# Two attention layers on one core: in layer 1, the k projection's left operands are loaded in one transfer at the start of a batch, and the next input's pieces move to other steps

## The chip, the cores and the metric

The kernel runs on one core of one Trainium2 chip. Its time is the device time of one execution in microseconds. It was timed in three runs; a profiled execution is a run of its own. Everything is in float32.

Five engines work at once and each runs its own instructions in order: TensorE (PE, matmuls; its weight loads are listed apart as PEld), VectorE (DVE), ScalarE (ACT), GpSimd (POOL) and SyncE (SP). SP computes nothing here: it issues nearly all DMAs, and a wait of one DMA holds up those behind it on SP. POOL issues a few DMAs of its own on another queue. All DMAs run on the core's 16 DMA engines.

## The reference

The input x is 8 images of 512 channels by 32 x 32 positions (T = 1024 tokens). Layer 0 is a group norm followed by an attention with 8 heads of 64 channels, a projection and a residual. Layer 1, in which the change lies, is, for each image:

```python
y = gn(x)                                            # group norm, 32 groups
q = einsum('oc,bct->bot', w_q, y)  # k and v likewise, then split in 8 heads of 64
attn = einsum('bhdq,bhdT->bhqT', q, k) * scale       # scores per head
attn = einsum('gh,bhqT->bgqT', w_head, attn)         # heads are mixed, 8 x 8
attn = softmax(attn, axis=-1)
attn = (attn - mean) / sqrt(var + eps) * in_gamma + in_beta   # mean, var over one head's whole map
out = einsum('bhqT,bhdT->bhqd', attn, v).reshape(b, t, c)     # no transpose: rows of heads stand as tokens
x = x + (out @ w_proj.T + b_proj) transposed back to (b, c, h, w)
```

## The kernel before

**Layer 0** runs first, for all 8 images, and writes its result to DRAM (`x1_d`). It also prepares the left operands of layer 1's projections: a projection of 512 x 512 weights with 512 x 1024 inputs is split in 2 x 2 blocks and done with 7 block products in place of 8 (`Projection`, order 1, 6, 2, 7, 5, 3, 4), and each product has a left operand that is a block of the weights or a sum of blocks. The 7 left operands of one projection lie side by side in DRAM (`left_d`), 128 partitions x 14 KB, 1792 KB in all. The layer 1 part uses the left operands as matrices w_t[key][:, f] with f = 0 to 6: product 1 takes f = 0, product 2 f = 1, product 6 f = 4, product 7 f = 5, product 5 f = 3, product 3 f = 6, product 4 f = 2.

**Layer 1** takes one image (batch b = 0 to 7) after another. For one batch, `Attention1.step(p, t, ag)` runs steps p = 0 to 8 with four quarters t = 0 to 3. Step p computes the raw scores of 128 queries for all 8 heads and 1024 keys (`scores`, 8 calls i = 0 to 7 with kh = i // 4 the half of the keys; PE at L1701, copied out of PSUM by ACT at L1713 or, in p = 0, partly by DVE at L1711). A copy goes to a tile `raw[kh]`, and SP regroups it with DMAs of 256 KB into `re_t` (`regroup`, L1719), so that heads lie beside each other on partitions; 16 such DMAs a step, 8 for each half, issued in quarters 1 to 3 (half 0 in t = 1 and 2, half 1 in t = 3). Step p + 1 mixes the heads of these scores (`mix(p, s)`, s = 0 to 3, one each quarter; PE at L1738, two PSUM tiles each), and ACT takes the exponential of each tile (L1751). DVE transposes (`flip`, L1766) and takes moments (`moments`, L1780). Step p + 2 multiplies with v (`values`, L1796) and ACT stores the result (`leave`, L1812). So at any time three steps' work is interleaved on PE, in the order in which the code writes it: the engines' order is the program's (a manual schedule), and waits are derived from which regions of which tiles are read and written.

The scores and the mixes draw their PSUM tiles from one pool of three buffers in turn (`m_psum`, pool ps1_m; a tile is two banks). Quarter 3 of a step that has both scores and mixes is, in code:

```python
self.scores(p, 6)
if old:
    self.values(p - 1, 0, 0)
self.scores(p, 7)
if old:
    self.mix(p - 1, 3)
    self.values(p - 1, 0, 1)
```

Work beside this is put into slots. `ag` (an Agenda) holds functions by slot number, and step (p, t) runs slot 4p + t at its very end (so slot 26 is the end of p = 6, t = 2), with a few slots in between (such as 4p + 1.5) inside the step. Functions that matter here:

- `y_piece(b + 1, c)` (L1376): DMA of one 128-channel quarter (512 KB) of the next batch's input into the tile y, c = 0 to 3. The tile has one buffer, and the current y is read by v projections up to p = 1.
- `left_piece` (L1345) and `load_left` (L1355): DMAs of left operands into a tile `left` of a pool with one buffer, which the projections share in turn; within a batch it holds the k operands of the next batch, then, after the k projection, the q operands of the next batch. `left_p` loads the output projection's operands into a `raw` buffer instead.
- `normalize1(b + 1, c)` (slots 24 to 27): group norm of one quarter of the next y in place; odd c on ACT (L704), even c on DVE (L708).
- `right_y` (slot 31.5, POOL, L1393): sums of blocks of y that are right operands of the products; `k_go` (slots 31.5, 32.5, ...): the next batch's k projection, products 1, 2, 6, 7 in p = 8, and 5, 4, 3 after it. p = 8 has no scores of its own.
- `totals` in odd p: row sums of two steps, from which DVE takes reciprocals; POOL writes them to DRAM (zd, L1844) and, for the even p that follows, reads them back broadcast over partitions (rzb, L1856, two DMAs of 256 KB each), then divides (L1883).

After p = 8 a batch finishes its last values, the rest of the next k projection, the output projection (`out1`) and the next q projection (`q_projection(b + 1).run()`), which is the last call of a batch's loop body. In the last batch there is no next one; its pieces are four 256 KB quarters of the plain output weights (`p_piece`) instead, also one each step.

A list `a.pieces` holds the pieces of a batch, and a step that calls `self.piece()` takes the next one. In the kernel before that is every step from p = 2 on, at the end of t = 0, ahead of the slot that ends that quarter.

Of the kernel before, what the change touches and what calls it, by code (L numbers as in the profile page):

```python
# [467 lines left out]
def tile_two_attention_layers(  # L468
# [19 lines left out]
    nc = tc.nc  # L488
# [4 lines left out]
    NT = T // P  # L493
# [812 lines left out]
    with ExitStack() as l1:  # L1306
# [31 lines left out]
                [P, 7, 2 * HC], F32, tag="left", name=f"left_{key[0]}_{key[1]}"  # L1338
            )

        def left_piece(key, f, n):

            if f == 0:
                left_tile(key)
            nc.sync.dma_start(  # L1345
                out=w_t[key][:, f : f + n].rearrange("p f o -> p (f o)"),
                in_=left_d[key[0] + "1"][:, 2 * f * HC : 2 * (f + n) * HC],
            )

        def load_left(key, t=None):  # L1350
            if t is None:
                left_tile(key)
# [334 lines left out]
        class Attention1:  # L1687
# [242 lines left out]
            def step(self, p, t, ag):  # L1930

                new, old, older = p < NT, p >= 1, p >= 2
                if t == 0:
                    if new:
                        for i in range(3):
                            self.scores(p, i)
                            if i == 1:
                                ag.run(4 * p - 0.75)
                    if older:
                        self.values(p - 2, 0, 2, 3)  # L1940
                        self.leave(p - 2, 0)
                        if p % 2:
                            self.sums(p // 2 - 1)
                    ag.run(4 * p - 0.5)
                    k_leave()
                    if old:
                        self.mix(p - 1, 0)
                    ag.run(4 * p - 0.25)
                    if p % 2 == 0 and p >= 4:
                        self.broadcast(0)  # L1950
                elif t == 1:
                    if older:
                        self.values(p - 2, 1, 0)
                        self.flip(p - 1, 0)
                        if p % 2:
                            self.totals(p // 2 - 1)
                        self.moments(p - 1, 0)
                    if new:
                        self.scores(p, 3)
                    ag.run(4 * p + 0.5)  # L1960
                    k_leave()
                    if old:
                        self.mix(p - 1, 1)
                elif t == 2:
                    if p % 2 == 0 and p >= 4:
                        self.broadcast(1)
                    if older:
                        self.values(p - 2, 1, 1)
                    if new:
                        self.scores(p, 4)  # L1970
                        self.scores(p, 5)
                    ag.run(4 * p + 1.5)
                    k_leave()
                    if old and not new:
                        self.mix(p - 1, 2)
                    if older:
                        self.values(p - 2, 1, 2, 3)
                        self.leave(p - 2, 1)
                    if old and new:
                        self.mix(p - 1, 2)  # L1980
                else:
                    if new:
# [7 lines that stand above are left out]
                    else:  # L1990
                        ag.run(4 * p + 2.5)
                        k_leave()
                        self.mix(p - 1, 3)
                        self.values(p - 1, 0, 0, 1)
                if p == 1 or old and t:
                    self.flip(p - 1, t)
                    self.moments(p - 1, t)
                if new:
                    first = 3 + (p == 0)
                    for kh, s in (  # L2000
                        [], [(0, i) for i in range(first)], [(0, i) for i in range(first, 4)],
                        [(1, i) for i in range(4)],
                    )[t]:
                        self.regroup(p, kh, s)
                if t == 3 and p % 2 == 0 and p >= 4:
                    self.divide(p // 2 - 2, nc.gpsimd)
                if older and t == 0:
                    self.piece()
                ag.run(4 * p + t)

# [22 lines left out]
        for b in range(B):  # L2033
            more = b + 1 < B
            a = Attention1(b)
            ag = Agenda()
            j = 2 * NV
            for slot, i, cs in (
                (-0.75, j, (0, 1)), (1, j, (2, 3)), (1, j + 1, range(NCC)), (3, j + 2, range(NCC)),
                (3.75, j + 3, (0, 1)), (5.5, j + 3, (2, 3)),  # L2040
            ):
                ag.at(slot, lambda i=i, cs=cs: v_tile(b, i, cs))
            if b == 0:
                stages = group_stages(B - 1, B, small_psum1)
                for i in range(3):
                    ag.at(i, stages[i])
                ag.at(3, v_sums)
            if more:
                a.pieces += [lambda c=c: y_piece(b + 1, c) for c in range(NCC)]
                a.pieces += [lambda f=f: left_piece(("k", b + 1), f, 2) for f in (0, 4)]  # L2050
                ag.at(4 * NT, lambda: left_piece(("k", b + 1), 2, 2))
                ag.at(4 * NT, lambda: left_piece(("k", b + 1), 6, 1))
                for c in range(NCC):
                    ag.at(24 + c, lambda c=c: normalize1(b + 1, c))

                def k_go(*ms):
                    if not kp:
                        kp.append(k_projection(b + 1))
                    for m in ms:
                        kp[0].products(m)  # L2060
                        due.append(lambda m=m: kp[0].leave(m))

                kp = []
                ag.at(4 * NT - 0.5, lambda: right_tile(b + 1))
                ag.at(4 * NT - 0.5, lambda: k_go(1))
                ag.at(4 * NT - 0.5, lambda: right_y(b + 1))
                ag.at(4 * NT + 0.5, lambda: k_go(2))
                ag.at(4 * NT + 1, lambda: left_p(b))
                ag.at(4 * NT + 1.5, lambda: k_go(6))
                ag.at(4 * NT + 2.5, lambda: k_go(7))  # L2070
            else:
                a.pieces += [lambda c=c: p_piece(c) for c in range(NCC)]

                def prelude():
                    out_products.extend(out1_last(a))
                    out_products[0](0, [0, 1])

                out_products = []
                ag.at(4 * NT - 0.5, prelude)
            for p in range(NT + 1):  # L2080
                for t in range(4):
                    a.step(p, t, ag)
            ag.flush()
            k_leave()
            last = NT - 1
            a.sums(NCH - 1)
            if not more:
                a.values(last, 0, 2, 3)
                a.leave(last, 0)
                out_products[0](0, [2])  # L2090
                out_products[0](1, [0, 1])
                out_products[2]()
                a.values(last, 1, 0, 1, 2, 3)
                a.leave(last, 1)
                a.totals(NCH - 1)
                a.broadcast(0)
                a.broadcast(1)
                a.instance()
                out_products[1]()
                continue  # L2100
            k_go(5)
            a.values(last, 0, 2, 3)
            a.leave(last, 0)
            load_wv(b + 1)
            a.values(last, 1, 0, 1, 2, 3)
            a.leave(last, 1)
            a.totals(NCH - 1)
            a.broadcast(0)
            a.broadcast(1)
            a.instance()  # L2110
            k_leave()
            k_go(4, 3)
            k_leave()
            a.instance_end()
            v_pair(b + 1, 0)
            a.divide(NCH - 1)
            for g in range(H):
                a.affine(g)
            right_o = re_t[:, 4:8]
            combine_right(right_o, out_view(b))  # L2120
            op = out1(b, right_o)
            load_left(("q", b + 1))
            v_pair(b + 1, 1)
            a.check()
            op.run()
            q_projection(b + 1).run()
# [57 lines left out]
```

## Time and profile before

| | us |
|---|---|
| three timed runs | 3902.49, 3907.03, 3908.03; median 3907.03 |
| the profiled execution's own time | 3899.99 |
| its span, first to last instruction | 3898.1 |
| TensorE matmuls busy | 3845.0 (99% of the span) |
| VectorE / ScalarE / GpSimd busy | 2840.8 / 1962.0 / 207.4 |
| q1, the queue of SP's DMAs | 500.48 MB, 45.3% of 16 engines' span |

TensorE's clock was granted at 0.999 of full speed in this execution. Layer 1's first score matmul starts at 1778 us; a batch of layer 1 takes about 270 us, a step about 21 us. The page lists for each group of instructions its busy time, the mean duration of one, and then the time that its engine was idle just before them with what ended most of that wait. Idle time counts only on the engine that bounds the stage. The timeline rows give start and duration, the engine, the line, the operation, the tiles (out<-in), the shapes and, in brackets, idle time before the row and its releaser; a releaser is the signal that came last by the records, and of several that lie close together it can be the wrong one. In names of tiles, m is a mix's PSUM tile, s a score's, re the regrouped scores, e the exponentials, a the values' PSUM tile, pq and pk the q and k projections'.

### The profile page before, as it was taken

Reading aid. Unit: us, or ns where it says so; the run is one execution under the profiler, and the core shown is the slowest. Engines: PE = TensorE matmul, PEld = TensorE weight load, DVE = VectorE, ACT = ScalarE, POOL = GpSimd, SP = SyncE. Lnnn points to the kernel's source line nnn. Section 1 sums busy time; section 2 is a strip of 40 time slices with the busy share of each in tenths; the row PEclk is TensorE's granted clock in tenths of the full one; section 3 lists DMA queues with packets and bytes.
Section 4 is the critical chain, followed back from the end, with each engine's and each line's share of the span. In section 5 each row is a group of like instructions: output and inputs, shape, how many; then the busy total and the mean of one; then the engine's idle time right before and its main releaser. Section 6 shows DMA issues by size and latency. Waiting matters only on the chain. (4 is left out here: it accounts for less than half of the span.)

```text
span 3898.1 us, 95183 instructions
## 1 busy us (share of the span) xinstructions
PE 3845.0 (99%) x41612; PEld 1809.6 (46%) x41612; DVE 2840.8 (73%) x3921; ACT 1962.0 (50%) x2400; POOL 207.4 (5%) x210
## 2 busy tenths in 40 slices
PE   8999999999999999999999999999999999999999
PEld 4353535344353535344554544545545545445455
DVE  4858586675859485866967958859769668678598
ACT  1726354453627172534826717528438257176175
POOL 0000000000000000000110200201101102002000
PEclk9999999999999999999999999999999999999999
DMA  3313131111122121216947929749659479297385
GB/s 122 123 52 118 50 113 43 67 67 71 58 73 67 59 81 49 91 47 162 235 133 194 231 91 232 194 127 240 180 136 239 150 171 237 96 222 206 119 222 161
DMA packets 248440, 519.45 MB, mean 133 GB/s; under 512 B 49872, under 2 KB 57040, under 8 KB 241360
## 3 DMA queue, kind: packets, MB, share of 16 engines
q1 hardware_dynamic: 240832, 500.48, 45.3%
q0 software_dynamic: 7184, 12.81, 1.6%
q8 instruction: 328, 5.37, 0.6%
q14 instruction: 96, 0.79, 0.1%
HBM read 197.16 MB, written 46.92 MB: 63 GB/s over the span
## 5 line engine op out<-in xcount | busy, mean ns | idle before, releaser
L1766 DVE STREAM_TRANSPOSE et<-e 128x2048 f32<-128x2048 f32 x256 | 590.0, 2305 | 190.4 <-ACT e L1751 189.3
L1796 PEld LDWEIGHTS a<-et,v 128*64 128x64 f32 x16384 | 505.7, 138 | 283.8 <-issue 266.1
L1780 DVE BATCH_NORM_STATS2 bn<-e 128x6 f32<-128x512 f32 x1024 | 635.7, 683 | 0.0
L1107 ACT ACTIVATE e<-s 128x1024 f32<-128x1024 f32 x512 | 496.9, 1024 | 233.0 <-PE s L1102 233.0
L1713 ACT COPY raw<-s 128x1024 f32<-128x1024 f32 x480 | 470.1, 1018 | 224.8 <-PE s L1701 201.3
L1751 ACT ACTIVATE e<-m 128x1024 f32<-128x1024 f32 x512 | 496.2, 1021 | 165.7 <-issue 62.4
L1796 PE MATMUL a<-et,v 128*64 128x64 f32 x16384 | 553.3, 224 | 0.0
L1701 PE MATMUL s<-k,q 64*64 64x512 f32 x4096 | 513.2, 605 | 2.7 <-DVE v L1060 1.4
L1102 PE MATMUL s<-q,k 64*64 64x512 f32 x4096 | 490.4, 594 | 2.3 <-ACT e L1107 2.3
L1117 DVE TENSOR_TENSOR zacc<-zacc,e 128x1024 f32<-128x1024 f32 x384 | 467.5, 1217 | 27.2 <-ACT e L1107 1.4
L1130 PE MATMUL a<-e,v 64*64 64x512 f32 x4096 | 484.1, 589 | 0.0
L1738 PE MATMUL m<-re,wmix 32*32 32x512 f32 x8192 | 306.2, 599 | 14.8 <-DMA re<-raw 11.8
L1130 PEld LDWEIGHTS a<-e,v 64*64 64x64 f32 x4096 | 156.7, 133 | 282.8 <-issue 282.5
L1102 PEld LDWEIGHTS s<-q,k 64*64 64x64 f32 x4096 | 146.2, 133 | 284.4 <-issue 220.2
L1844 POOL DMA_DIRECT2D zd<-rz x96 | 52.5, 552 | 3361.9 <-DMA y<-x 1846.6
L1701 PEld LDWEIGHTS s<-k,q 64*64 64x64 f32 x4096 | 127.2, 132 | 216.0 <-issue 95.5
L1812 ACT COPY q<-a 64x256 f32<-64x256 f32 x256 | 94.0, 367 | 138.7 <-PE a L1796 137.1
L1738 PEld LDWEIGHTS m<-re,wmix 32*32 32x32 f32 x8192 | 68.1, 103 | 154.3 <-ACT raw L1713 65.9
L1509 PE MATMUL pv_t<-wv,y 128*128 128x512 f32 x256 | 120.6, 609 | 0.0
L920 PE MATMUL pv_p<-left_v,tmp 128*128 128x256 f32 x512 | 113.1, 379 | 0.0
L920 PE MATMUL pk_p<-tmp,left_k 128*128 128x512 f32 x256 | 112.5, 592 | 0.0
L920 PE MATMUL pq_p<-tmp,left_q 128*128 128x512 f32 x256 | 112.5, 592 | 0.0
(332 smaller groups left out, 3918.3 us busy)
## 6 DMA issues: line engine op xcount, KB each, us to landing
re<-raw SPq DMA_DIRECT2D x1024, 256.0 KB
left_q<-left_q SPq DMA_DIRECT2D x17, 1792.0 KB
left_p<-left_p SPq DMA_DIRECT2D x17, 1792.0 KB
left_k<-left_k SPq DMA_DIRECT2D x10, 1792.0 KB
x<-in_x_dram SPq DMA_DIRECT2D x32, 512.0 KB
rzb<-zd SPq DMA_DIRECT2D x128, 128.0 KB
x<-x SPq DMA_DIRECT2D x64, 256.0 KB
y<-x SPq DMA_DIRECT2D x32, 512.0 KB
```

Source lines behind the costliest of these rows:

```text
L920: nc.tensor.matmul(out, st, mv, start=start, stop=(k == 1), skip_group_check=True)
L1102: nc.tensor.matmul(ps[c * D : c * D + D, m], k[r, hp, k0 : k0 + D], q[r, hp, ts(f, FB)], start=True, stop=True,)
L1107: nc.scalar.activation(e[i], ps, AF.Exp, scale=S0 * S0)
L1117: nc.vector.tensor_add(zacc[g], zacc[g], e[i])
L1130: nc.tensor.matmul(acc[g][a][m * D : m * D + D], v[rows, kc, ts(2 * hp + m, D)], e[i][rows, m], start=(kc == 0), stop=(kc == NG - 1),)
L1701: nc.tensor.matmul(ps[c * D : c * D + D, m], qo_t[b][r, p, hp, ts(c, D)], k_t[b][r, hp, ts(kh, FB)], start=True, stop=True,)
L1713: nc.scalar.copy(dst, ps)
L1738: nc.tensor.matmul(ps[a // 2][c * 32 : c * 32 + 32, a % 2].rearrange("p (r h k) -> p h r k", r=2, h=2), wmix[rows].rearrange("p g i -> p ( ...
L1751: nc.scalar.activation(e[:, :, 2 * h : 2 * h + 2].rearrange("p r a k -> p a r k"), ps[h].rearrange("p a (r k) -> p a r k", r=2), AF.Exp,)
L1766: nc.vector.transpose(self.et[p, u].rearrange("p kb (r st a) g q -> p st kb r (a g q)", r=2, st=2)[:, st], self.e[p, s].rearrange("p r a ( ...
L1780: nc.vector.bn_stats(self.bn[n][:, p % 2, s, a], e[:, :, a].rearrange("p r k -> p k r"))
L1796: nc.tensor.matmul(acc[two * D : two * D + D, s].rearrange("p (x q) -> p x q", q=4), v_t[b][:, kb, ts(g, D)], et[:, kb, :, g], start=(kb = ...
```

## The change

Three edits, all in layer 1's loop.

1. The k operands of the next batch are no longer loaded in four pieces (two of 512 KB from the list of pieces, then 512 KB and 256 KB at slot 32). One `load_left(("k", b + 1))` of 1792 KB is issued where the batch's loop body sets up its agenda, ahead of the first step. `left_piece` goes.
2. `piece()` is called in t = 0 of p = 2, 4, 6 and 7 (the third, fifth, seventh and eighth step) in place of every p from 2 on. So the four quarters of the next input, which went out in p = 2, 3, 4 and 5, go out in p = 2, 4, 6 and 7; in the last batch the same holds for the weights' quarters.
3. The normalizations of quarters 0 to 3 stand in slots 24, 25, 26 and 30 in place of 24, 25, 26 and 27. Quarter 3 is one of ACT's.

```diff
-        def left_piece(key, f, n):
-
-            if f == 0:
-                left_tile(key)
-            nc.sync.dma_start(
-                out=w_t[key][:, f : f + n].rearrange("p f o -> p (f o)"),
-                in_=left_d[key[0] + "1"][:, 2 * f * HC : 2 * (f + n) * HC],
-            )
...
-                if older and t == 0:
+                if t == 0 and p in (2, 4, 6, 7):
                     self.piece()
                 ag.run(4 * p + t)
...
             if more:
                 a.pieces += [lambda c=c: y_piece(b + 1, c) for c in range(NCC)]
-                a.pieces += [lambda f=f: left_piece(("k", b + 1), f, 2) for f in (0, 4)]
-                ag.at(4 * NT, lambda: left_piece(("k", b + 1), 2, 2))
-                ag.at(4 * NT, lambda: left_piece(("k", b + 1), 6, 1))
+                load_left(("k", b + 1))
                 for c in range(NCC):
-                    ag.at(24 + c, lambda c=c: normalize1(b + 1, c))
+                    ag.at((24, 25, 26, 30)[c], lambda c=c: normalize1(b + 1, c))
```

## The prediction

> **What bounds the kernel now.** I read the page first, then the groups of instructions by line, then the timelines of PE, ACT and SP around the places that the change touches, and for DMAs the completion records (semaphore updates) in the trace. Steps are counted p = 0 to 8 as in the code, quarters t = 0 to 3; the third, fifth, seventh and eighth step are p = 2, 4, 6 and 7.
>
> The page's busy times say that TensorE is the bound:
>
> ```profile
> PE 3845.0 (99%) x41612; PEld 1809.6 (46%) x41612; DVE 2840.8 (73%) x3921; ACT 1962.0 (50%) x2400; POOL 207.4 (5%) x210
> ```
>
> Only 53 us of the 3898.1 us span have no matmul in flight, so an edit can win little, and any new hole in PE costs its full length. The groups say which part of the holes has to do with the loads: the mixes wait for regrouped scores.
>
> ```profile
> L1738 PE MATMUL m<-re,wmix 32*32 32x512 f32 x8192 | 306.2, 599 | 14.8 <-DMA re<-raw 11.8 <-ACT q L1812 1.8 <-ACT raw L1713 0.4
> ```
>
> The PE timeline of batch 1 (b = 1) places them: the mix that opens p = 4 and the one that opens p = 6 have idle time before them (last bracket), the one that opens p = 5 (middle line) none.
>
> ```profile
> 2139.65 1.15 PE L1738 MATMUL m<-re,wmix 32*32 32x512 f32 x32 [0.60 <-DMA re<-raw]
> ...
> 2160.16 1.14 PE L1738 MATMUL m<-re,wmix 32*32 32x512 f32 x32
> ...
> 2181.91 1.15 PE L1738 MATMUL m<-re,wmix 32*32 32x512 f32 x32 [0.87 <-ACT q L1812]
> ```
>
> The 0.87 is also a DMA's: its regroup landed at 2181.77 by the completion records. Read off in the same way, the holes at p = 4 and p = 6 are, by batch from 0: 0.90 and 0.99, 0.60 and 0.87, 1.12 and 0.67, 0.45 and 0.47, 0.38 and 0.17, 1.76 and 0.50, 0.59 and 1.65, and in the last batch 1.10 and 0.32. Batches 0 to 6 sum to 11.1 us (0.79 a hole), the last to 1.4. Why there: in p = 3 and p = 5 the POOL queue also sends the broadcast of reciprocals, and it meets the second half of the regroups. POOL's timeline in p = 3, issues first, then the wait for their landing:
>
> ```profile
> 2130.80 1.12 POOL L1856 DMA_DIRECT2D rzb<-zd  x2 [4.29 <-DMA re<-raw]
> 2138.16 2.36 POOL L1883 TENSOR_TENSOR q<-q,rzb 128x1024 f32<-128x1024 f32 x1 [6.23 <-DMA rzb<-zd]
> ```
>
> These steps move 4 MB of regroups (16 of 256 KB), 0.5 MB of input and 0.5 MB of broadcast in 21 us. The windows' DMA share is 0.96 in 2119.70:2133.20 and 1.05 in 2133.20:2141.20.
>
> **The change part by part.**
>
> *The input piece leaves p = 3 and p = 5* (it goes to p = 4 and p = 6; p = 2 keeps its own; p = 6 and 7 lose 512 KB of left operands and get 512 KB of input). So only p = 3, 5 and 8 carry less. What does the hole become? A step opens 5.76 us after the second half's first regroup was issued when nothing stalls, and the pair it needs must land by about 5.64. In p = 3 and 5 of batches 0 to 6 that pair landed after 5.87 to 7.46 us, mean 6.49. The trace has one step with the broadcast at that place and no piece at all, p = 7 of the last batch: 6.22, a hole of 0.58 by the 5.76 rule. The last batch's half-size pieces (256 KB of weights) leave 1.10 and 0.32, mean 0.71. And batches 3 and 4, whose broadcasts were issued 2.4 to 3.5 us ahead of the half, have 0.37. I take 0.5 after the change, between these rows: batches 0 to 6 gain 14 x 0.29 = 4.1 us, the last 2 x 0.21 = 0.4; together 4.5. Bounds: 0 (the broadcast alone makes the hole) and 12.5 (all go); a loss is excluded, these steps only shed traffic. p = 8 loses 768 KB, but no mix of p = 8 in batches 0 to 6 waited for a DMA: 0.
>
> The Trainium skill, "DMA: Bandwidth & Descriptors", section "Queues, rings and completion order", says that each DMA engine takes turns between the queues that have work, packet by packet. By it the broadcast keeps taking half of the engines from the regroups whatever is removed from SP's queue, the hole stays and the sum is 4.5 us worse; the 6.22 without a piece against the mean of 6.49 with one stands between that and full relief, and I keep the row.
>
> *Normalization of the fourth input piece moves from slot 27 (end of p = 6, t = 3) to slot 30 (end of p = 7, t = 2).* Pieces 1 and 3 are on ACT, so this is an ACT instruction (1.24 us, L704) put between the exponentials of the third mix and the copy of score 6. ACT and PE timelines there, now:
>
> ```profile
> 2212.89 0.74 ACT L1812 COPY q<-a 64x256 f32<-64x256 f32 x2 [0.93 <-PE a L1796]
> 2214.11 1.94 ACT L1751 ACTIVATE e<-m 128x1024 f32<-128x1024 f32 x2 [0.48 <-ACT q L1812]
> 2215.94 1.02 ACT L1713 COPY raw<-s 128x1024 f32<-128x1024 f32 x1
> 2217.11 1.01 ACT L1713 COPY raw<-s 128x1024 f32<-128x1024 f32 x1 [0.16 <-PE s L1701]
> 2218.32 1.94 ACT L1751 ACTIVATE e<-m 128x1024 f32<-128x1024 f32 x2 [0.19 <-PE m L1738]
> ```
>
> ```profile
> 2215.96 1.09 PE L1701 MATMUL s<-k,q 64*64 64x512 f32 x8
> 2216.98 1.17 PE L1738 MATMUL m<-re,wmix 32*32 32x512 f32 x32
> ```
>
> ```profile
> 2216.97 0.26 PEld L1738 LDWEIGHTS m<-re,wmix 32*32 32x32 f32 x32 [0.81 <-ACT raw L1713]
> ```
>
> The copy of score 6 ends at 2216.96 and the fourth mix starts at 2216.98. This is no coincidence of numbers: ps1_m has 3 buffers; score 6, score 7 and the mix's first half fill them, so its second half needs the buffer that the copy of score 6 empties. The slack is 0.0 us. ACT cannot have run ahead either: it waits for PE's values (0.93) and then for the mix just before. Put in, the instruction took 1.13 us from start to next start at slots 25 and 27 (2188.66 to 2189.80, 2199.00 to 2200.13). The copy of score 6 then ends at 2218.09, the mix's third matmul, due at 2217.01, waits 1.08 us: 7 batches x 1.08 = 7.6 us on PE. Queued behind on ACT are copies 6 and 7; copy 7 releases SP's second half of regroups (2218.15), 1.0 later, and the mix that needs these is itself 1.1 later. What follows in p = 8 is PE back to back, with nothing to take the shift up. Bounds: 0 (ACT finds time) and 7 x 1.24 = 8.7. I take 7.6 since both engines' times stand in the rows. At the old slot nothing is won: after 2199.00 come three copies, and the opening mix at 2202.84 had 0.01 of idle time.
>
> *The input is there in time.* Piece 2 is issued about 2181.5 and normalized on DVE at 2199.57 (slot 26, unchanged); piece 3 about 2203.3, used about 2216. The 512 KB pieces now issued at these places took 9.0 and 7.5 us to land (completion records); margins 9 and 5 us: 0. POOL's combination of right operands (2219.76) waits for a raw tile's regroups and stays after the new normalization (2217.2): 0.
>
> *The left operands of k as one DMA as the batch begins.* SP takes it up when the last q product frees the tile: PE's last pq matmul of batch 0 ends at 2055.85, SP's next issue is the first regroup. SP's timeline:
>
> ```profile
> 2033.11 0.37 SPq L1584 DMA_DIRECT2D out_dram<-xs  x1
> 2062.88 6.38 SPq L1719 DMA_DIRECT2D re<-raw  x8
> ```
>
> 7.03 us lie between (the same in all seven batches after batch 0), and before it the DMA engines are empty (share 0.01 in 2055.90:2062.90). Nothing else is queued behind the wait. The same 1792 KB as left_q took 5.5 to 7.0 us of packets, and as left_p its packets began 1.2 to 1.9 us after issue; so the last packet is 6.7 to 8.9 us after the issue,  I take 0. Upper bound: left_p landed 8.7 to 10.2 us after issue. A regroup held back 1.6 us eats a slack of 0.5 (pair landed 4.30, needed by about 4.8) and costs 1.1 x 6 batches = 6.6 us. In batch 0 the first mix comes 20 us after the first regroup: 0. Fewer issues on SP (4 to 1) free time on a queue that is not late: 0.
>
> The Trainium skill, "DMA: Bandwidth & Descriptors", section "Anatomy of one DMA — SWDGE (gpsimd) path", fits 2.0 us plus bytes over 436 GB/s for a DMA of POOL's kind: 6.2 us here as an estimate, over before the first regroup, and the sum would be the same without any risk. The rows (8.7 and more) are slower than that fit, so the bound above stays.
>
> *Sum*: -4.5 + 7.6 + 0 = +3.1 us. The profiled execution took 3899.99 us (span 3898.1), 7 below the median of the timed runs; its 3903.1 after the change means 3910 against the median of 3907.03. About 0.2% (7.8 us) is what a measurement can tell from no change, so this is "within", on the slow side.
>
> **The rivals.**
> 1. The broadcast alone makes the holes: no relief. For it: 6.22 without a piece, 1.10 with half a piece. Against: the two longest waits (7.46, 7.34) came with full pieces. 3907.0 + 7.6 = 3914.6. Chance 0.20.
> 2. Slower through the batch's start: the big load delays the first regroups, the mix opening p = 1 stalls in six batches; it decides from 0.5 us of delay on. 3910.1 + 6.6 = 3916.7. For it: landing rows beyond 7.03. Against: packets end before. 0.09.
> 3. Faster: ACT's insertion hides and the holes shrink: 3902.5, or 3894.5 if they go. Against: slack 0.0 and three buffers. 0.08.
> 4. The holes all go, and ACT costs as said: 3907.0 - 12.5 + 7.6 = 3902.1. For it: p = 5, with its neighbour's piece but no broadcast, has nearly no hole. Against: the broadcast stays. 0.08.
>
> **How the numbers follow.** My forecast has 0.55. Timed medians move by some 3 us. Below 3899.2 (faster): most of rival 3 and a little of 4, 0.07. Above 3914.8: half of rival 1, nearly all of 2, and 0.08 of the forecast's own spread, 0.26. Within: 0.67. From 3900 to 3918 the range takes in rivals 1, 2 and 4 and leaves out part of 3.
>
> **What would show it.** Right: one left_k issue about 0.1 us after the last pq matmul; in p = 7 the fourth mix with about 1.1 us idle, released by ACT's copy, in seven batches; holes at p = 4 and 6 near 0.5; the mix group's idle time near 18 us in place of 14.8. Wrong: no hole at that mix (the ACT step), holes at p = 4 and 6 unchanged or gone (the relief), idle time at the mix that opens p = 1 (the load).

## The result, and the profile after

The changed kernel took 3914.45 us in the median of 13 runs (3907.36 to 3921.71); the kernel before, run beside it, took 3905.13 us (13 runs, 3900.20 to 3913.31). The ratio of the times is 1.0021, with a 95% interval from 1.0014 to 1.0029: slower by 8.2 us (5.5 to 11.3); the two medians themselves lie 9.3 us apart. The profiled execution took 3911.54 us (span 3909.8 us) against 3899.99 before, 11.6 us more. The granted clock was 0.999 in both, so the clock has no part in it.

The page of the changed kernel, busy times of the engines:

```profile
PE 3851.9 (99%) x41612; PEld 1810.7 (46%) x41612; DVE 2841.2 (73%) x3921; ACT 1962.7 (50%) x2400; POOL 207.1 (5%) x210
```

The number of matmuls is the same to the last one, yet PE is busy for 6.9 us more. The groups of the changed kernel, the mixes (the copy of raw scores, `raw`, is L1704 here, the mix L1729, the exponential L1742, `leave` L1803):

```profile
L1729 PE MATMUL m<-re,wmix 32*32 32x512 f32 x8192 | 310.8, 599 | 18.7 <-DMA re<-raw 11.4 <-ACT raw L1704 3.5 <-ACT q L1803 2.5
```

Busy time of the mixes rose from 306.2 to 310.8 us, idle time before them from 14.8 to 18.7 us. Two places account for most of the slowdown.

**The fourth mix of p = 7.** ACT's timeline of the changed kernel around it, batch 1:

```profile
2215.13 0.74 ACT L1803 COPY q<-a 64x256 f32<-64x256 f32 x2 [0.93 <-PE a L1787]
2216.35 1.94 ACT L1742 ACTIVATE e<-m 128x1024 f32<-128x1024 f32 x2 [0.48 <-ACT q L1803]
2218.18 1.24 ACT L704 ACTIVATE y<-y,gneg,grstd 128x1024 f32<-128x1024 f32 x1
2219.31 1.93 ACT L1704 COPY raw<-s 128x1024 f32<-128x1024 f32 x2
```

PE's timeline at the same place, score 7 and the mix:

```profile
2218.20 1.09 PE L1692 MATMUL s<-k,q 64*64 64x512 f32 x8
2219.22 2.29 PE L1729 MATMUL m<-re,wmix 32*32 32x512 f32 x32
```

The normalization (L704) stands where the copy of score 6 used to start, and the copy starts 1.13 us later. The mix of 32 matmuls, 1.17 us before, now lasts 2.29: its first half has a buffer, its second waits for the copy. Of each wait the records list only 0.11 us as idle time, too little for a bracket in these rows; the rest is counted as busy time of the mix. In batches 0 to 6 the row is 2.29 or 2.30 in every batch: 7 x 1.13 = 7.9 us. Measured as the distance between the mix that opens p = 7 and the one that opens p = 8, the seven steps p = 7 together went from 152.88 to 160.62 us, 7.7 us more.

**The holes before the mixes that open p = 4 and p = 6.** PE's timeline of the changed kernel, the mixes that open p = 3, 4 and 6 of batch 1:

```profile
2120.03 1.15 PE L1729 MATMUL m<-re,wmix 32*32 32x512 f32 x32 [0.19 <-DMA re<-raw]
...
2141.65 1.15 PE L1729 MATMUL m<-re,wmix 32*32 32x512 f32 x32 [0.73 <-DMA re<-raw]
...
2184.47 1.15 PE L1729 MATMUL m<-re,wmix 32*32 32x512 f32 x32 [1.44 <-DMA re<-raw]
```

They did not shrink. Over batches 0 to 6 the two holes sum to 14.3 us against 11.1 before, in the last batch to 1.0 against 1.4. The input piece is gone from p = 3 and p = 5; the regroup pair that the opening mix needs landed on average 6.72 us after the half's first issue, 6.49 before.

**The load as the batch begins** behaves as its issue suggests. SP's timeline of the changed kernel:

```profile
2057.48 0.34 SPq L1346 DMA_DIRECT2D left_k<-left_k  x1
2064.48 26.16 SPq L1710 DMA_DIRECT2D re<-raw  x24
```

The idle time of the mix that opens p = 1 sums to 0.49 us over the batches, 0.48 before.

From the start of the first mix to the start of the last, layer 1 grew from 2049.0 to 2060.2 us: 11.2 us, of which 7.7 are the step p = 7 and 2.8 the holes (3.2 more in batches 0 to 6, 0.4 less in the last).

### The profile page after: what moved, and what is told of

It reads as the page before. It is cut to its first block, busy times and chain, and to the rows that moved or that the text cites. A ratio compares the mean times of both kernels' runs of the same rounds, so it can differ in the third digit from the quotient of the medians.

```text
span 3909.8 us, 95138 instructions
## 1 busy us (share of the span) xinstructions
PE 3851.9 (99%) x41612; PEld 1810.7 (46%) x41612; DVE 2841.2 (73%) x3921; ACT 1962.7 (50%) x2400; POOL 207.1 (5%) x210
## 5 line engine op out<-in xcount | busy, mean ns | idle before, releaser
L1704 ACT COPY raw<-s 128x1024 f32<-128x1024 f32 x480 | 469.4, 1018 | 223.5 <-PE s L1692 195.6
L1742 ACT ACTIVATE e<-m 128x1024 f32<-128x1024 f32 x512 | 496.3, 1021 | 169.5 <-issue 62.3
L1729 PE MATMUL m<-re,wmix 32*32 32x512 f32 x8192 | 310.8, 599 | 18.7 <-DMA re<-raw 11.4
L1803 ACT COPY q<-a 64x256 f32<-64x256 f32 x256 | 94.0, 367 | 146.4 <-PE a L1787 144.8
L1729 PEld LDWEIGHTS m<-re,wmix 32*32 32x32 f32 x8192 | 68.4, 103 | 163.1 <-ACT raw L1704 71.0
```

The costliest lines, as they stand in the source:

```text
L1704: nc.scalar.copy(dst, ps)
L1729: nc.tensor.matmul(ps[a // 2][c * 32 : c * 32 + 32, a % 2].rearrange("p (r h k) -> p h r k", r=2, h=2), wmix[rows].rearrange("p g i -> p ( ...
L1742: nc.scalar.activation(e[:, :, 2 * h : 2 * h + 2].rearrange("p r a k -> p a r k"), ps[h].rearrange("p a (r k) -> p a r k", r=2), AF.Exp,)
```

## The experiments

Each kernel was timed in five rounds beside the kernel before. Three questions lead through them: is the 7.7 us the normalization's place, why did the relief fail to come, and does the early load cost anything.

### The normalization's new slot alone (norm30)

The kernel before, with one edit.

```diff
                 for c in range(NCC):
-                    ag.at(24 + c, lambda c=c: normalize1(b + 1, c))
+                    ag.at((24, 25, 26, 30)[c], lambda c=c: normalize1(b + 1, c))
```

> The kernel before with one edit: the normalization of the fourth input quarter, an instruction of ScalarE, moves from slot 27 to slot 30. Theory A (the loss is this instruction, which delays the copy of score 6 and with it the fourth mix of p = 7): seven batches x 1.1 us, 7 to 8.5 us slower than before (ratio 1.0018 to 1.0022), the fourth mix of p = 7 lasts about 2.3 us in place of 1.17 in seven batches. Theory B (the loss comes from the DMAs: the new places of the pieces and the large load lengthen the holes at p = 4 and p = 6, which summed to 11.1 us before and 14.3 after in batches 0 to 6): at most 4 us slower, holes as before.

Measured: 3913.96 us (11 runs) against 3907.96 (27 runs), ratio 1.0016 [1.0007, 1.0025], 2.7 to 9.8 us slower. ACT's timeline, batch 1:

```profile
2216.15 1.94 ACT L1751 ACTIVATE e<-m 128x1024 f32<-128x1024 f32 x2 [0.48 <-ACT q L1812]
2217.98 1.24 ACT L704 ACTIVATE y<-y,gneg,grstd 128x1024 f32<-128x1024 f32 x1
2219.11 1.93 ACT L1713 COPY raw<-s 128x1024 f32<-128x1024 f32 x2
```

And PE's:

```profile
2218.00 1.09 PE L1701 MATMUL s<-k,q 64*64 64x512 f32 x8
2219.02 2.29 PE L1738 MATMUL m<-re,wmix 32*32 32x512 f32 x32
```

The same order on ACT and the same 2.29 us: the steps p = 7 sum to 160.82 us, 7.9 above before. One moved instruction accounts for the larger part of the slowdown.

This kernel's DMAs have the order of before, and its holes at p = 4 and p = 6 still sum to 14.2 us in batches 0 to 6, as after the change. So a sum between 11 and 14 us is nothing that the change of the pieces made.

### The change with its normalization one slot later (after31)

The edit is to the changed kernel. Slot 31 ends p = 7, after the copies of scores 6 and 7.

```diff
                 for c in range(NCC):
-                    ag.at((24, 25, 26, 30)[c], lambda c=c: normalize1(b + 1, c))
+                    ag.at((24, 25, 26, 31)[c], lambda c=c: normalize1(b + 1, c))
```

> The changed kernel with the same normalization one quarter later, in slot 31 (end of p = 7, t = 3), where copies of scores no longer follow. Theory A: the fourth mix of p = 7 is back at 1.17 us and the time is that of before, ratio 0.9990 to 1.0008 with the sign set by what the moved pieces do to the holes. Theory B: still 3 to 8 us slower than before.

Measured: 3905.37 us (11 runs) against 3907.96, ratio 1.0000 [0.9991, 1.0009]. ACT's timeline, batch 1: the copy of score 7, the exponentials, and the normalization behind them:

```profile
2218.07 1.02 ACT L1704 COPY raw<-s 128x1024 f32<-128x1024 f32 x1
...
2220.45 1.94 ACT L1742 ACTIVATE e<-m 128x1024 f32<-128x1024 f32 x2 [0.19 <-PE m L1729]
2222.28 1.24 ACT L704 ACTIVATE y<-y,gneg,grstd 128x1024 f32<-128x1024 f32 x1
```

PE's, the fourth mix:

```profile
2219.11 1.17 PE L1729 MATMUL m<-re,wmix 32*32 32x512 f32 x32
```

The mix is back at 1.17 us and the steps p = 7 at 153.65. With ACT's loss gone, what is left is what the pieces and the load do together: nothing that can be measured. A gain of 4.5 us, the relief that was forecast, would be a ratio of 0.9988 and lies just outside the interval. The holes at p = 4 and p = 6 sum to 12.0 us in batches 0 to 6, between the 11.1 and the 14.3 of the two kernels.

### The pieces moved in the kernel before (even24)

In batches 0 to 6 the input goes out in pairs in p = 2 and p = 4, and none in p = 3 and p = 5; nothing else is changed.

```diff
-                if older and t == 0:
-                    self.piece()
+                if older and t == 0 and not (self.b + 1 < B and p in (3, 5)):
+                    self.piece(2 if self.b + 1 < B and p in (2, 4) else 1)
```

> The kernel before with the input pieces of batches 0 to 6 two at a time in p = 2 and p = 4 and none in p = 3 and p = 5; all else stays. The forecast's relief: the holes that open p = 4 and p = 6 shrink from 0.79 to about 0.5 us, 4 us faster (ratio 0.9990). Rival (POOL's broadcast alone makes these holes, the piece has drained long before): holes stay near 0.8, ratio 0.9997 to 1.0005, or a little slower if the double pieces make new holes at the openings of p = 3 and p = 5.

Measured: 3912.12 us (11 runs) against 3907.96, ratio 1.0009 [1.0000, 1.0018]. SP's timeline, the pairs of batch 1 with no piece between them:

```profile
2103.74 1.34 SPq L1376 DMA_DIRECT2D y<-x  x2
2106.07 38.50 SPq L1719 DMA_DIRECT2D re<-raw  x32
2144.61 1.53 SPq L1376 DMA_DIRECT2D y<-x  x2
```

PE's, the openings of p = 4 and p = 6:

```profile
2145.27 1.15 PE L1738 MATMUL m<-re,wmix 32*32 32x512 f32 x32 [0.96 <-DMA re<-raw]
...
2188.90 1.15 PE L1738 MATMUL m<-re,wmix 32*32 32x512 f32 x32 [1.24 <-ACT raw L1713]
```

The 1.24 is a DMA's too, though the row names ACT: by the completion records the pair that this mix needs landed at 2188.76. With both steps free of input, the holes sum to 14.1 us in batches 0 to 6: no relief, a second time. The pairs cost something of their own where they stand: from the opening of p = 2 to that of p = 3 seven batches took 148.17 us in place of 143.99, and from p = 4 to p = 5 148.65 in place of 145.40.

### The broadcast taken away (nobcast)

The kernel before without POOL's two broadcasts of reciprocals and its division in p = 4, 6 and 8.

```diff
-                    if p % 2 == 0 and p >= 4:
-                        self.broadcast(0)
...
-                    if p % 2 == 0 and p >= 4:
-                        self.broadcast(1)
...
-                if t == 3 and p % 2 == 0 and p >= 4:
-                    self.divide(p // 2 - 2, nc.gpsimd)
```

> The kernel before without POOL's two broadcasts of reciprocals and its division in p = 4, 6 and 8 of every batch: this part of the softmax's division is left out, the rest is computed. If the broadcast's transfers in p = 3 and p = 5 make the holes that open p = 4 and p = 6, these go altogether although the input pieces stay where they were: 10 to 13 us faster (ratio 0.9967 to 0.9975). If the pieces make them: holes of 0.5 us and more stay, at most 4 us faster.

Measured: 3886.76 us (5 runs, 3886.08 to 3890.11) against 3907.96, ratio 0.9950 [0.9936, 0.9963]. Its mixes in the groups:

```profile
L1738 PE MATMUL m<-re,wmix 32*32 32x512 f32 x8192 | 305.6, 599 | 2.2 <-DMA re<-raw 1.3 <-ACT e L1751 0.4 <-issue 0.2
```

PE's timeline, the openings of p = 4 and p = 6 of batch 1, with no idle time before them:

```profile
2140.00 1.14 PE L1738 MATMUL m<-re,wmix 32*32 32x512 f32 x32
...
2181.52 1.14 PE L1738 MATMUL m<-re,wmix 32*32 32x512 f32 x32
```

Pieces and regroups are where they were, and the holes at p = 4 and p = 6 are gone: 0.1 us in batches 0 to 6. So the broadcast is necessary for the holes and the piece is not sufficient for them. (POOL's division goes with it here, but it stays in the experiment on SP's queue below, where the holes go as well.) The profiled execution took 3890.04 us, 10 less than that of before, about the 12.5 us of holes. The ratio of the medians is worth 20 us, more than was expected. The profiled execution of before lay 8.0 us below its median and that of this kernel 3.3 above; what an execution of before spends these 8 us on no profile shows, and what the left-out work itself is worth was not taken apart.

### The load at the start alone (loadstart)

The kernel before, with its four pieces of left operands replaced by the one load.

```diff
-                a.pieces += [lambda f=f: left_piece(("k", b + 1), f, 2) for f in (0, 4)]
-                ag.at(4 * NT, lambda: left_piece(("k", b + 1), 2, 2))
-                ag.at(4 * NT, lambda: left_piece(("k", b + 1), 6, 1))
+                load_left(("k", b + 1))
```

> The kernel before with one edit: the k operands in one load as the batch begins; input pieces (p = 2 to 5) and normalizations (slots 24 to 27) stay, so p = 6, 7 and 8 carry less. If the load lies in the free stretch before the first regroups: no idle time before the mix that opens p = 1 beyond what before shows (0.3 to 0.5 us in one batch), ratio 0.9995 to 1.0005. If it holds the first regroups back: 1 us at that mix in six batches, 4 to 7 us slower (1.0010 to 1.0018).

Measured: 3905.82 us (12 runs) against 3906.64 (23 runs), ratio 0.9996 [0.9986, 1.0006]. SP's timeline:

```profile
2057.35 0.34 SPq L1355 DMA_DIRECT2D left_k<-left_k  x1
2064.35 26.16 SPq L1719 DMA_DIRECT2D re<-raw  x24
```

7.00 us lie between the load and the first regroup, and the openings of p = 1 have 0.45 us of idle time in all. By the completion records the load landed 7.1 to 8.5 us after its issue, here and in the changed kernel, so in part after the first regroup was issued, and the mix waited no longer than before. The load is free, and the four pieces that it replaces cost nothing measurable either. The holes at p = 4 and p = 6, here with the input pieces in p = 3 and p = 5, sum to 12.7 us in batches 0 to 6.

### The broadcast on SP's queue (spbcast)

If the holes come from the broadcast that meets the second half's regroups from another queue, it should help to send it in order ahead of them. In the kernel before, SP issues the two broadcasts at the end of the first quarter of p = 4 and p = 6; p = 8 keeps POOL's. The edit changes two things at once: the queue, and the time, which is 10 to 12 us later than POOL's in batch 1 and behind the late regroups.

```diff
-                self.zq.dma_start(
+                queue = nc.sync if self.zn < 2 else self.zq
+                queue.dma_start(
...
                         self.broadcast(0)
+                        if p < NT:
+                            self.broadcast(1)
...
-                    if p % 2 == 0 and p >= 4:
+                    if p == NT:
                         self.broadcast(1)
```

> The kernel before with POOL's broadcast of p = 4 and p = 6 issued by SP in t = 0 of the same step, both halves together, so behind the regroups of the step before and not among them. If what makes the holes at p = 4 and p = 6 is that the broadcast on its own queue takes DMA time from the regroups just issued: these holes go (sum of batches 0 to 6 from 11 to 14 us down to under 2). The broadcast then stands beside a 512 KB piece in p = 4 and p = 6, as the doubled pieces did, which cost about 0.5 us at the next opening: 14 x 0.5 = 7 us. Net 4 to 8 us faster (0.9980 to 0.9990). If it is the sum of the traffic and not its order: holes move from p = 4 and 6 to p = 5 and 7 in full, ratio 0.9997 to 1.0003.

Measured: 3912.79 us (12 runs) against 3906.64, ratio 1.0018 [1.0009, 1.0028]. A miss: the holes at p = 4 and p = 6 are gone (0.1 us), and the kernel is slower. In batches 0 to 6 the steps p = 3 and p = 5, from opening mix to opening mix, are 9.9 us shorter than before, and p = 4 and p = 6, which hold broadcast and piece, 19.7 us longer. The waits of PE in layer 1 (engine, tile, line, what was waited for: us in total, times, longest):

```profile
PE a L1796 <- issue: 4.3, 8, 1.3
PE m L1738 <- issue: 3.1, 4, 1.8
PE s L1701 <- issue: 2.8, 3, 1.6
```

"Issue" means that the engine waited for nothing that the profile shows. The kernel before has 0.3 us of it here. PE's timeline shows one such wait, in the middle of a group of values, after 61 of its 64 matmuls:

```profile
2191.35 2.02 PE L1796 MATMUL a<-et,v 128*64 128x64 f32 x61
2194.66 0.33 PE L1796 MATMUL a<-et,v 128*64 128x64 f32 x3 [1.29 <-issue]
```

SP's timeline a few us before:

```profile
2184.51 1.67 SPq L1857 DMA_DIRECT2D rzb<-zd  x2
2186.22 0.58 SPq L1345 DMA_DIRECT2D left_k<-left_k  x1
```

The broadcast (512 KB) and the step's piece (512 KB) now follow each other on one queue, and the regroups behind them land 7.9 to 8.9 us after issue (first six after 2188). In before the six at this place (issued from 2186.27 to 2190.51) took 5.0 to 5.6. The busy times of this kernel's page:

```profile
PE 3857.0 (99%) x41612; PEld 1812.2 (46%) x41612; DVE 2839.8 (73%) x3921; ACT 1963.8 (50%) x2400; POOL 189.4 (5%) x178
```

12 us more busy time for the same matmuls is again waiting inside groups. So the 11 us won at the holes were paid back, and more, as issue waits and as waits in mid-group.

### Broadcast and piece kept apart (best)

If it is the two together that cost, the change's freedom to choose the steps of the pieces can be used to keep them apart. This is the changed kernel with the edit of the last experiment, the normalization in slot 31, and no piece in p = 4 and p = 6.

```diff
-                if t == 0 and p in (2, 4, 6, 7):
+                if t == 0 and p in (2, 3, 5, 7):
                     self.piece()
...
-                    ag.at((24, 25, 26, 30)[c], lambda c=c: normalize1(b + 1, c))
+                    ag.at((24, 25, 26, 31)[c], lambda c=c: normalize1(b + 1, c))
```

> The changed kernel with three edits: the broadcasts of p = 4 and p = 6 issued by SP in t = 0 as in the run beside it, the input pieces in p = 2, 3, 5 and 7 (the steps without a broadcast on SP), and the last normalization in slot 31. No step then has both a piece and a broadcast in the same quarter. If order and place of the transfers make the holes: openings of p = 4 to 7 under 0.2 us each, 10 to 14 us faster than before (0.9964 to 0.9974). If the steps are bound by the sum of traffic: 0 to 5 us faster.

Measured: 3889.29 us (6 runs, 3888.23 to 3890.03) against 3906.64, ratio 0.9957 [0.9944, 0.9970]: 17 us faster than before, and better than both kernels. (The profiled execution took 3888.23 us, 11.8 less than that of before, about the 12.1 us by which the holes shrank, 0.4 being left of 12.5 with the last batch counted. As with the broadcast taken away, the medians lie further apart than that.) SP's timeline, batch 1, the broadcast in p = 4 and the piece in p = 5:

```profile
2139.90 1.82 SPq L1848 DMA_DIRECT2D rzb<-zd  x2
2143.50 17.24 SPq L1710 DMA_DIRECT2D re<-raw  x16
2160.79 0.79 SPq L1367 DMA_DIRECT2D y<-x  x1
```

The mixes in layer 1's groups:

```profile
L1729 PE MATMUL m<-re,wmix 32*32 32x512 f32 x8192 | 304.5, 599 | 3.3 <-DMA re<-raw 2.4 <-ACT e L1742 0.3 <-issue 0.2
```

And the page's busy times:

```profile
PE 3843.9 (99%) x41612; PEld 1808.4 (47%) x41612; DVE 2839.6 (73%) x3921; ACT 1963.6 (51%) x2400; POOL 189.4 (5%) x178
```

PE's issue waits in layer 1 are 0.8 us, the holes at p = 4 and p = 6 sum to 0.4, and busy time is 1.1 us below that of before. The early load makes room for this: in the kernel before, four pieces of input and two of left operands take all six steps from p = 2 to p = 7.

### The same with the change's own steps (sp2467)

The last kernel, with the pieces in the steps that the change gives them.

```diff
-                if t == 0 and p in (2, 3, 5, 7):
+                if t == 0 and p in (2, 4, 6, 7):
                     self.piece()
```

> The faster kernel (broadcasts of p = 4 and p = 6 on SP, load at the start, last normalization in slot 31) with one edit: the input pieces back in p = 2, 4, 6 and 7, so that p = 4 and p = 6 have a broadcast and a piece one behind the other in SP's queue and p = 3 and p = 5 neither. If two such transfers in one quarter are what made the run with only the broadcast moved slower: waits of TensorE named issue come back (10 us there, under 1 us in the faster kernel) and the time is that of the kernel before or above it, ratio 0.9995 to 1.0020. If the place of the pieces has no part in it: 0.9945 to 0.9970 as in the faster kernel.

Measured: 3909.76 us (11 runs) against 3907.68 (15 runs), ratio 1.0009 [1.0000, 1.0018]. The waits of PE in layer 1:

```profile
PE m L1729 <- issue: 3.3, 6, 1.6
PE a L1787 <- issue: 2.6, 5, 1.0
...
PE s L1692 <- issue: 1.3, 3, 0.6
```

Only the steps of the pieces differ from the kernel of 3889.29 us. 7.2 us of issue waits are back, PE's busy time is 3855.0 us, and 20 us are lost. In batches 0 to 6 p = 4 and p = 6 take 16.3 us more than in that kernel. The pieces in these steps cost nothing while the broadcast was on POOL's queue (after31, ratio 1.0000), so it is broadcast and piece in one quarter of SP's queue that costs.

## Why the prediction was right and wrong

The forecast was 3910.0 us, +3.1 on the median; measured was +8.2 (5.5 to 11.3), an interval that leaves +3.1 out. The range held the time because it was drawn wide enough for three of the rivals, and the side was right, but what happened is rival 1, "The broadcast alone makes the holes: no relief", with its +7.6 (3914.6). Of the two large terms one was right and one was not, so that the range held is in part luck.

- **ACT's insertion, +7.6: right.** Predicted was 1.08 us in seven batches for want of a PSUM buffer; the mix grew by 1.13 us in each of them, 7.7 to 7.9 us, and both experiments on the slot (30 alone, 31 in its place) show the cause. The sign announced was imprecise: of the "about 1.1 us idle" only 0.11 us is listed as idle time, the rest lies inside the mix's own row.
- **The relief, -4.5: this is the step that failed.** No relief was measured. The prediction took the 0.79 us holes to 0.5 because "only p = 3, 5 and 8 carry less". The holes did not shrink in three kernels without input in p = 3 and p = 5: 14.3, 12.0 and 14.1 us in batches 0 to 6, against 11.1 before and 14.2 and 12.7 in norm30 and loadstart, which have the input where it was. What was overlooked stands in the trace of before. SP's timeline, batch 1, the piece and the regroups of p = 3:

```profile
2119.69 0.66 SPq L1376 DMA_DIRECT2D y<-x  x1
2122.95 16.98 SPq L1719 DMA_DIRECT2D re<-raw  x16
```

By the completion records the piece had landed at 2127.28, and the second half's regroups, the last eight of the row, were issued only from 2133.22 on: it was gone from the queue 6 us before the regroups that were late. In p = 3 and p = 5 of batches 0 to 6 it was gone 5.7 to 7.6 us before them, all fourteen times. The broadcast, issued at 2130.80, landed at 2137.99, right among them. The prediction compared steps by what they move in 21 us, where here only the few us ahead of the late transfer mattered. The one row without a piece, 6.22, was taken as relief against a mean of 6.49; at the same place, with the same transfers in that batch, norm30, loadstart and even24 have 6.82, 7.06 and 8.00, so the row showed no relief but one draw from a spread.
- **The Trainium skill's rule against it.** "DMA: Bandwidth & Descriptors", section "Queues, rings and completion order", says that each DMA engine takes turns between the queues that have work, packet by packet. The prediction drew from it that the broadcast keeps its share whatever leaves SP's queue, gave this 4.5 us on the worse side and kept its own row. What it drew from the rule came true: the holes stay when the input leaves (14.1 us), and go when the broadcast leaves (0.1) or is issued later and on SP's queue (0.1). The packets agree that the two queues share the engines: in the first 3 us after the second half's first issue, mean of the fourteen steps, POOL's queue, which carries the broadcast, moved 335 KB and SP's 315 KB; with the broadcast left out SP's moved 410 KB. The pair that the mix needs landed 6.49 us after that issue on average, and 4.68 without the broadcast. No run sends the broadcast on SP's queue at its old time, so turns between the queues are not told apart from the mere amount of traffic at that moment.
- **The load at the batch's start, +0: right.** Alone it measures 0.9996 [0.9986, 1.0006]. The load landed up to 1.5 us after the 7.03 us of free queue were over, and the mixes at p = 1 waited no longer than before; the 6.6 us of the upper bound did not come.
- **The check by "idle time near 18 us" came true for the wrong reason.** It is 18.7, but with holes of 14.3 us in batches 0 to 6 (not 7) and only 0.8 of ACT's 7.9. A sum that fits is no proof of its terms.
- **"Only 53 us of the 3898.1 us span have no matmul in flight"** read PE's busy time as matmuls alone. It holds waits in mid-group too: with the same matmuls it was 3843.9 us in one kernel and 3857.0 in another.

The expectation of the broadcast on SP's queue mis-sized a term in its turn: broadcast and piece side by side were priced at 7 us, and p = 4 and p = 6 grew by 19.7 us, since PE's issue, which no term held, was late as well.

What stays open: the profiled holes differ by some 3 us between executions with the same DMAs in these steps (11.1 and 14.2), and why is not known. The 3.2 us by which the profiled holes of the changed kernel exceed those of before can be such a difference, since after31 with the same DMAs has 12.0.

## What to carry to other kernels

Where an engine waits for a transfer, list by completion times what is in flight at that moment, on all queues; here the input that had landed 6 us before the late transfers were issued had no measurable part in the wait, though it is as many bytes as the broadcast that had. Before an instruction is put into an engine that is mostly idle, look for what it stands in front of: with three buffers taken in turn, one copy 1.13 us later held the matmuls up by as much in each batch. And two transfers that were each harmless in a step of their own cost 20 us here when they were queued one behind the other in the same steps, so their places are chosen together.

## What the runs showed of the hardware that was not expected

- **Waits in the middle of a group count as busy time.** With 41612 matmuls in each case PE's busy time was 3843.9, 3845.0, 3851.9, 3855.0 and 3857.0 us in five of the kernels. Where it grows with the same work and clock, look for long rows in the timeline.
- **PE's issue waits end behind packets of the instruction queue.** They sum to 10.2 us in spbcast and 7.2 in sp2467, against 0.8 in the fastest kernel, all with the same matmuls in the same order. The trace has a queue of its own for instructions, with packets of 16 KB some 6.3 us apart in the median. All 29 issue waits of spbcast and sp2467 ended 1.2 to 1.6 us after the end of such a packet. Set row by row against the fastest kernel, PE's starts in layer 1 fall behind by 19.0 us in sp2467; of the jumps of over 0.2 us, 26.6 us in all (some of it is won back), 15.5 us come 1.2 to 1.75 us after the end of such a packet, a stretch that holds about a sixteenth of the time. In spbcast it is 21.4 of 32.9 us; in the kernel before, set against the same kernel, 1.7 of 18.1. So the traces say that PE waited for its instructions, beyond the waits that are listed as issue; no run varied the fetching itself, and why these packets came late is not shown. "Runtime: NRT & Kernel Launch", section "Instruction fetch mechanics", of the Trainium skill says that instructions come in blocks of 16 KiB over a DMA queue of the engine's own and that this is mostly hidden. The packets agree with the size, and in these two kernels it was not hidden.
- **The spread of the times went with the losses.** The kernel before ranged over 12.4 us in one set of 27 runs (3901.90 to 3914.31). It is not the holes alone: spbcast, without them but with the issue waits above, ranged over 11.9 us in 12 runs. Without the broadcast five runs lie within 4.0 us, and with broadcast and piece kept apart six lie within 1.8 us (3888.23 to 3890.03).
